# Recurrent layer: second column sums and GpSimd's output copies moved ahead in the order

## Chip, cores and metric

One NeuronCore of a Trainium2 chip runs the whole program in one launch. The metric is the device time of that launch in microseconds, the median of several runs. The profile is one execution of the same program; its page names the engines PE (TensorE), DVE (VectorE), ACT (ScalarE), POOL (GpSimd) and SP (SyncE, which here issues nearly all DMAs).

## The reference

The input is `x`, 128 sequences of 64 steps of 256 features, in float32, with a 64 x 64 adjacency. Four residual layers follow each other, each closed by a layer norm: a graph attention, a second graph attention over 512 edges, a graph layer with two batch norms, and the one that this case concerns, a recurrent layer over a two-step graph convolution:

```
h = relu(adj @ (x @ Wg0 + bg0)); h = relu(adj @ (h @ Wg1 + bg1))
for p in (1, 2, 3, 4):
    wins = windows of p successive steps of h          # 64 // p per sequence
    last = LSTM_p(wins, zero start state), last hidden state
    h[:, last step of each window] = last
x = layernorm(x + h)
```

An LSTM step has gates i, f, g, o, each 256 wide, from `x_t @ Wih.T + h @ Whh.T + bias`; `c = sigmoid(f) c + sigmoid(i) tanh(g)`, `h = sigmoid(o) tanh(c)`. Lengths p = 1 to 4 run one after the other on the same `h`, so each sees what the shorter ones wrote.

## The kernel before

**Tiling.** The recurrent layer handles the 128 sequences in eight groups of 16, two groups to a pair, four pairs one after the other (`k` = 0 to 3). A pair's activations are one tile `H` (128 partitions, two groups, two halves of the features, 64 steps, 16 sequences). `gcn` builds a pair's half-group of `H` in some eight steps, the last of which writes `H` (L1347, L1348).

**Products.** Where it can, the kernel computes a gate's 2 x 2 block product with seven products in place of eight, which needs sums of the inputs' blocks. For p = 1, `column_sums(n)` (L1389 to L1394) makes four such sums of group n, 128 x 512 each, on GpSimd, into the tile `Tn[n]`, which shares a buffer with weights (`wx`). `Wide` runs p = 1: gate g of group 0 takes all eight products (`eight`, L1505) and needs no sums; the other five gates take seven (`seven`, L1437), in the order 1, 6, 5, 2, 3, 7, then 4 during the next gate. Products 6, 7 and 4 share a bank of PSUM, so 7 cannot start before VectorE has read 6, nor 4 before it has read 7. The instructions that are issued through the helper `given` have its line, L116, in the profile. For p > 1, `Gate` does the same (L1700) with `hsums` and `xsums`; product uses are at L1711 to L1728, gates' activations at L1733, cell and hidden products at L1597 to L1622. Six banks (`l`) hold products on their way from TensorE to VectorE and ScalarE.

**Order.** `lstm` is a generator that yields numbered units: 0 to 7 for p = 1, 8 to 21 for p = 2, 22 to 32 for p = 3, 33 to 47 for p = 4. Beside it stands a table (`put`) of side work: at each unit the loop at the end (L1927 to L1930) advances the parts that are due there. Side parts are `gcn` of the next pair, `prepare` (loads of weights), and `final`. `given` ties each part's instructions behind those before it on each engine, so the order on an engine is nearly that of the text. In pairs 1 and 2, a layer norm of `gcn` for the pair after follows unit 0: on VectorE L1292 to L98, on GpSimd L86 and L100.

**Outputs.** `final(g, s)` turns step s (of every four) of group g into an output. For s = 0, 1, 2, which p = 4 does not write, it copies the columns with two GpSimd instructions into a tile `hd` (L1835), loads the residual rows (`x3r`, L1843), transposes blocks on VectorE (L1236 in `turned`), sends the result through DRAM (`way`, L1239, and back, L1241), and yields. Its second step, two units on, adds the residual (L1850), normalises and stores (L1860). The first steps stand at units 34, 36, 38, 40, 42, 44, the two groups in turn. For s = 3 the columns come straight from VectorE's last products (L1591).

[...]A transpose at L1236 is followed on VectorE by gate work, and a copy at L1835 on GpSimd by the forget gate's product with the cell (L1610) or by a layer norm (L86, L100).

Of the kernel before, what the change touches and what calls it, by code (L numbers as in the profile page):

```python
# [41 lines left out]
def kernel(ctx: ExitStack, tc: tile.TileContext, i, out):  # L42
# [45 lines left out]
    def layernorm(dst, src, n, engine):  # L88

        st = small.tile([P, n, 6], F32, name="ln_st", bufs=5)  # L90
        mv = small.tile([P, n, 2], F32, name="ln_mv", bufs=5)
        both = small.tile([P, 2, n], F32, name="ln_rs", bufs=5)
        rs, ng = both[:, 0, :], both[:, 1, :]
        for r in range(n):
            nc.vector.bn_stats(st[:, r, :], src[:, r, :])  # L95
            nc.vector.bn_aggr(mv[:, r, :], st[:, r, :])
        rsqrt(rs, mv[:, :, 1], n)
        nc.vector.tensor_scalar_mul(ng, mv[:, :, 0], -1.0)  # L98
        for r in range(n):
            engine.tensor_scalar(dst[:, r, :], src[:, r, :], ng[:, r:r + 1], rs[:, r:r + 1],  # L100
                                 op0=OP.add, op1=OP.mult)
# [8 lines left out]
    def given(do, *args, **more):  # L110
        traced = nc.cur_bb.bb.instructions
        first = len(traced)
        with ExitStack() as order:
            for e in latest.values():
                order.enter_context(tc.issue_after(e))
            r = do(*args, **more)  # L116
        for t in traced[first:]:
            if t.engine in (mybir.EngineType.PE, mybir.EngineType.DVE, mybir.EngineType.Activation,
                            mybir.EngineType.Pool):
                latest[t.engine] = t  # L120
        return r
# [8 lines left out]
    with ExitStack() as two:  # L130
# [450 lines left out]
        pair = su.tile([P, EC, 4], F32, name="pair")  # L581
# [154 lines left out]
        def hidden(q, m):  # L736
            return Z[q][:, m, :] if m < 2 else Aq(q)[:, (m - 2) * QT:(m - 1) * QT]
# [15 lines left out]
        def put(q, m, p_):  # L753
            nc.scalar.activation(hidden(q, m), p_, AF.Identity, bias=b1[:, m:m + 1])
            nc.vector.bn_stats(st1[:, m, q, :], hidden(q, m))
# [405 lines left out]
    def gbank(shape):  # L1161
        return ps.tile([P] + shape, F32, name="g", bufs=2)
# [69 lines left out]
    def turned(src):  # L1232


        t = work.tile([P, 4, 4, 32], F32, name="st", bufs=ST)
        nc.vector.transpose(t, src.rearrange("p n (j t) -> p j n t", t=32))  # L1236
        o = work.tile([P, 4, 4, 32], F32, name="st", bufs=ST)
        way = dram.tile([P, 4, P], F32, name="way", bufs=4)
        nc.sync.dma_start(way, t.rearrange("p j n f -> p j (n f)"))  # L1239
        for j in range(4):  # L1240
            nc.sync.dma_start(o[j * 32:(j + 1) * 32].rearrange("t i n f -> t i (n f)"),  # L1241
                              way[:, j, :].rearrange("(i t) x -> t i x", t=32))
        return o.rearrange("p i (c m) f -> p c m i f", m=KD)
# [132 lines left out]
    def lstm(pair):  # L1376
# [123 lines left out]
        def eight(G, rest):  # L1500

            def two(m, v):
                b = lbank([QT])
                for k in range(KD):
                    nc.tensor.matmul(b, G.weight(m, k), half(G.n, k, v), start=k == 0, stop=k == KD - 1)  # L1505
                return b

            for m in range(2):
                for v in range(2):
                    G.act(m, v, given(two, m, v))  # L1510
                    next(rest, None)
            for _ in rest:
                pass

        def seven(G, rest, order):
            for j in order:
                G.product(j)
                next(rest, None)
            for _ in rest:
                pass  # L1520

        rest = iter(())
        for n in range(2):
            if n == 0:
                given(column_sums, 0)
                yield "begin", 0
            gates = {}
            for name in "gio":
                if (n, name) == (0, "o"):
                    given(column_sums, 1)  # L1530
                G = Wide(name, n, gates)
                if name == "g" and n == 0:
                    eight(G, rest)
                    rest = iter(())
                else:
                    seven(G, rest, (1, 6, 5, 2, 7, 3) if (n, name) == (1, "o") else (1, 6, 5, 2, 3, 7))
                    rest = G.tail()
                if (n, name) == (1, "o"):
                    G.last()
                yield "at", unit  # L1540
                unit += 1
            yield "at", unit
            unit += 1

        for p in range(2, SKIP + 1):
# [197 lines left out]
            for r in range(len(runs)):  # L1743
                if p > 2:
                    yield "gap", unit
                for s in range(p):
# [16 lines left out]
                    else:  # L1763
# [31 lines left out]
                        o = prev  # L1795
# [32 lines left out]
    def final(g, s, pieces=1):  # L1828

        if s == SKIP - 1:  # L1830
            h = lasts.pop(g)
        else:
            h = late.tile([P, 2, KD, P], F32, name="hd", bufs=3)
            for c in range(2):
                nc.gpsimd.tensor_copy(h[:, c].rearrange("p k (w b) -> p k w b", b=GB),  # L1835
                                      Hs[g // 2][:, g % 2].rearrange("p k (c w s) b -> p c k w s b",
                                                                     c=2, s=SKIP)[:, c, :, :, s, :])

        rows = [v[g * GB:(g + 1) * GB].rearrange("b (c w s) d -> s c w b d", c=2, s=SKIP)[s]
                for v in (x3_dram, out_view)]  # L1840
        xr = work.tile([P, 2, D], F32, name="x3r")
        for c in range(2):
            nc.sync.dma_start(xr[:, c, :], rows[0][c])  # L1843
        for cs in ([(0, 1)] if pieces == 1 else [(0,), (1,)]):
            r = slice(cs[0], cs[-1] + 1)
            if pieces == 1:
                ht = turned(h.rearrange("p c m t -> p (c m) t"))
                yield
                xv = xr.rearrange("p c (m i f) -> p c m i f", m=KD, f=32)
                nc.vector.tensor_add(xv, ht, xv)  # L1850
            else:
                ht = gbank([2, D])
                for c in cs:
                    for k in range(KD):
                        nc.tensor.transpose(ht[:, c, k * P:(k + 1) * P], h[:, c, k], ident)
                nc.vector.tensor_add(xr[:, r], ht[:, r], xr[:, r])
            o = work.tile([P, 2, D], F32, name="st", bufs=ST)
            layernorm(o[:, r], xr[:, r], len(cs), nc.gpsimd)
            for c in cs:
                nc.sync.dma_start(rows[1][c], o[:, c, :])  # L1860
        yield
# [9 lines left out]
    for n in [0, 0, 0, 1, 1, 0, 1, 0, 0, 1, 2, 0, 0, 2, 1, 2, 1, 0, 3, 1, 1, 1]:  # L1871
        given(next, parts[n])
    lstms = [lstm(k) for k in range(NP)]
    next(lstms[0])
    for n in [2, 3, 2, 3, 2]:
# [18 lines left out]
    def gap(u):  # L1894
        return "gap", u

    def wait(u):
        return "wait", u

    for k in range(NP):  # L1900
        if k:
            put(k, prepare(weights_of[k, 3]), 8)
            put(k, prepare(weights_of[k, 4]), 23)
        else:
            put(k, prepare(weights_of[k, 4]), 23, 26, 30)
        for n in range(2):
            g = k * 2 + n
            for s in range(SKIP - 1):
                u = 34 + 4 * s + 2 * n
                put(k, final(g, s), u, u + 2)  # L1910
            if k < NP - 1:
                put(k + 1, final(g, SKIP - 1), 9 + n, 12 + n)
        if k < NP - 1:
            put(k, prepare(weights_of[k + 1, 2]), 34)
            for n, keys in enumerate([
                    [9, gap(11), 12, wait(15), 16, gap(18)],
                    [5, 9, 11, 13, 15, 19, wait(22), gap(22), gap(25), 26, gap(29)],
                    [13, 17, 19, 21, 23, 27, wait(33), gap(33), gap(36), 37, 38],
                    [21, 24, 26, 28, 30, 34, gap(40), 41, gap(44), 45, 46]]):
                block = gcn((k + 1) * 2 + n // 2, n % 2, gbank, "hT")  # L1920
                if n == 0 and k:
                    put(k - 1, block, 40, 42, 43)
                    put(k, block, 0, 0)
                elif n == 0:
                    put(k, block, 0, 1, 3, 5, 7)
                put(k, block, *keys)
# [5 lines left out]
    for n in (1, 0):  # L1932
        for _ in final((NP - 1) * 2 + n, SKIP - 1, pieces=2):
            pass
# [40 lines left out]
```

## Time and profile before

| | us |
|---|---|
| median of 3 runs | 2052.08 |
| lowest, highest | 2048.62, 2052.64 |
| profiled execution, its own time | 2051.53 |
| its span, first to last instruction | 2049.7 |
| TensorE busy | 1943.6 (95%) |
| VectorE busy | 1256.3 (61%) |
| ScalarE busy | 987.6 (48%) |
| GpSimd busy | 883.8 (43%) |

Pair 0's p = 1 starts at some 796 us of the span (its first column sum), pairs 1, 2 and 3 begin at 1133, 1445 and 1756 us. A line of a timeline gives start, duration, engine, source line, operation, the tile written and those read, the shapes, how many such instructions stand together, and in brackets how long the engine stood idle before it and what released it. A line of the waits gives who waited, for whom, the total in us, how often, and the longest. Two neighbouring matrix products overlap at their ends, so the time lost at a gap is read from start to start; the gap itself is a little shorter. Mean granted TensorE clock was 0.986 of full speed.

### The profile page before, as it was taken

What the parts mean: (1) busy time and instruction counts of PE and PEld (TensorE: products, weight loads), DVE (VectorE), ACT (ScalarE), POOL (GpSimd) and SP (SyncE); (2) the same over time, 40 slices, a digit from 0 to 9 for tenths busy, and PEclk for the clock granted to TensorE, in tenths of its full rate; (3) what the DMA queues carried; (4) which work ended last, traced back from release to release, by engine and by line L of the source; (5) the groups of instructions that cost most, each with busy time, mean ns of one, the idle gap of its engine ahead of it and who ended that gap; (6) DMA issues with size and microseconds to landing.
All of it is one profiled execution on the core that took longest, in us unless ns stands there. A gap on an engine that the chain in (4) does not pass through costs nothing.

```text
span 2049.7 us, 31505 instructions
## 1 busy us (share of the span) xinstructions
PE 1943.6 (95%) x11447; PEld 1332.9 (65%) x11447; DVE 1256.3 (61%) x2763; ACT 987.6 (48%) x1892; POOL 883.8 (43%) x1017
## 2 busy tenths in 40 slices
PE   5999999999899989899999999999999999999997
PEld 4666667766454435477677477677577667578685
DVE  7456665564457454765566865556775557764566
ACT  2766667666335633634343644343544333544333
POOL 1123334343345543564545543435443445444264
PEclk8999999999999999999999999999999999999998
DMA  5344443332112125432242243132143032131022
GB/s 134 79 65 68 79 69 54 66 50 39 37 29 60 41 103 171 158 136 98 112 143 85 77 140 139 42 126 91 52 153 120 21 113 65 44 119 78 0 65 70
DMA packets 236539, 173.84 MB, mean 85 GB/s; under 512 B 150624, under 2 KB 213600, under 8 KB 233056
## 3 DMA queue, kind: packets, MB, share of 16 engines
q1 hardware_dynamic: 234528, 169.86, 29.1%
q8 instruction: 90, 1.47, 0.3%
q0 software_dynamic: 1024, 1.05, 0.2%
q10 hardware_dynamic: 832, 0.92, 0.1%
q14 instruction: 65, 0.53, 0.1%
HBM read 110.18 MB, written 61.60 MB: 84 GB/s over the span
## 4 chain that ended last, share of the span: by engine, by line
PE 68%; DVE 17%; ACT 5%; POOL 4%; issue 4%; DMA 1%; SPq 0%; DVEq 0%; POOLq 0%; ACTq 0%
PE l L1700 25%; PE l L1656 7%; PE l L1437 4%; PE pz L820 4%; PE e L346 3%; PE m L318 2%; PE pz L749 2%; PE g L1336 2%; PE m L253 2%; PE m L321 2%; PE z L355 2%; PE pz L1017 2%; PE g L1324 2%; DVE ln_st L95 1%; DVE cell L1614 1%
## 5 line engine op out<-in xcount | busy, mean ns | idle before, releaser
L1700 PE MATMUL l<-xs,wx 128*128 128x256 f32 (+1 forms) x896 | 277.0, 400 | 5.7 <-DVE gate L1719 4.2
L1700 PE MATMUL l<-hs,wh 128*128 128x256 f32 (+1 forms) x896 | 276.5, 399 | 2.9 <-DVE hs L1564 2.1
L1715 ACT ACTIVATE kept<-l 128x256 f32<-128x256 f32 (+1 forms) x224 | 88.6, 402 | 332.2 <-PE l L1700 330.7
L86 POOL TENSOR_TENSOR ln_rs<-ln_rs,mhalf 128x2 f32<-128x2 f32 (+2 forms) x98 | 86.4, 882 | 338.1 <-DVE ln_rs L98 334.9
L1700 PE MATMUL l<-H,wx 128*128 128x256 f32 (+1 forms) x672 | 210.5, 402 | 4.3 <-DVE gate L1728 3.4
L1700 PE MATMUL l<-hid,wh 128*128 128x256 f32 (+1 forms) x672 | 208.8, 399 | 0.0
L1700 PEld LDWEIGHTS l<-xs,wx 128*128 128x128 f32 x896 | 168.6, 190 | 50.7 <-issue 5.8
L1700 PEld LDWEIGHTS l<-hs,wh 128*128 128x128 f32 x896 | 169.2, 190 | 46.8 <-DVE hs L1564 4.7
L1733 ACT ACTIVATE gate<-gate,bias 128x512 f32<-128x512 f32 (+1 forms) x280 | 170.6, 657 | 42.0 <-DVE gate L1724 34.8
L1656 PE MATMUL l<-H,wx 128*128 128x256 f32 (+5 forms) x672 | 185.2, 431 | 4.9 <-DVE H L116 2.7
L1656 PEld LDWEIGHTS l<-H,wx 128*128 128x128 f32 x672 | 118.8, 190 | 65.5 <-issue 34.2
L357 ACT ACTIVATE u<-z 128x1024 f32<-128x1024 f32 x128 | 130.3, 1025 | 63.4 <-PE z L355 62.6
L1700 PEld LDWEIGHTS l<-H,wx 128*128 128x128 f32 x672 | 125.7, 190 | 42.6 <-DVE gate L1728 7.4
L1700 PEld LDWEIGHTS l<-hid,wh 128*128 128x128 f32 x672 | 127.2, 190 | 32.0 <-issue 2.6
L1723 POOL TENSOR_TENSOR gate<-gate,kept 128x256 f32<-128x256 f32 (+1 forms) x84 | 64.9, 773 | 154.2 <-DVE kept L1721 153.9
L329 DVE TENSOR_TENSOR qs<-m,qs 64x256 fp32r<-64x256 f32 x128 | 54.1, 422 | 109.1 <-ACT qs L328 107.0
L355 PE MATMUL z<-gath_r,qs 128*128 128x512 f32 x256 | 99.9, 478 | 0.6 <-ACT u L357 0.4
L1622 ACT ACTIVATE gate<-cell 128x512 f32<-128x512 f32 (+1 forms) x88 | 58.6, 666 | 86.5 <-DVE cell L1614 64.5
L1568 POOL TENSOR_TENSOR hs<-hid 128x256 f32<-128x256 f32 (+1 forms) x28 | 27.4, 977 | 168.3 <-DVE hid L1600 85.2
L1728 DVE TENSOR_TENSOR gate<-l,gate 128x256 f32<-128x256 f32 (+1 forms) x112 | 50.0, 446 | 61.4 <-POOL gate L1723 36.4
L1610 POOL TENSOR_TENSOR cell<-gate,cell 128x512 f32<-128x512 f32 (+1 forms) x56 | 75.4, 1367 | 28.4 <-ACT gate L1733 28.4
L1717 DVE TENSOR_TENSOR gate<-l,kept 128x256 f32<-128x256 f32 (+1 forms) x112 | 49.2, 439 | 57.1 <-ACT gate L1733 32.9
(375 smaller groups left out, 4095.3 us busy)
## 6 DMA issues: line engine op xcount, KB each, us to landing
wx<-sums SPq DMA_DIRECT2D x9, 2048.0 KB
wh<-sums SPq DMA_DIRECT2D x9, 1792.0 KB
way<-st SPq DMA_DIRECT2D x54, 256.0 KB
st<-way SPq DMA_DIRECT2D x216, 64.0 KB
xin<-in_x SPq DMA_DIRECT2D x16, 512.0 KB
ld<-table SPq DMA_DIRECT2D x16, 512.0 KB
x_dram<-y SPq DMA_DIRECT2D x16, 512.0 KB
x2r<-x_dram SPq DMA_DIRECT2D x32, 256.0 KB
```

Source lines behind the costliest of these rows:

```text
L86: nc.gpsimd.tensor_tensor(dst, dst, mhalf[:, :n], OP.pow)
L346: nc.tensor.matmul(pes[S][n * CG:(n + 1) * CG, :], apad[:, k, CG - HEADS - r0:2 * CG - HEADS - r0], u[:, k, :], start=r0 == 0 and k == 0, ...
L355: nc.tensor.matmul(z[:, k, :], L1[q]["qs"][c][:, s, k * P:(k + 1) * P], gath_r, start=True, stop=True)
L357: nc.scalar.activation(u, z, AF.Relu)
L820: nc.tensor.matmul(self.bank[at], lhs, rhs, start=first and n == 0, stop=n == len(self.terms) - 1, skip_group_check=True)
L1437: nc.tensor.matmul(self.bank[at], lhs, rhs, start=new, stop=True, skip_group_check=True)
L1610: nc.gpsimd.tensor_tensor(c, t, c, OP.mult)
L1656: nc.tensor.matmul(b, w.raw[0][:, k, at, m, :], x, start=k == 0, stop=k == KD - 1)
L1700: nc.tensor.matmul(self.banks[j], lhs, rhs, start=src == 0, stop=src == 1)
L1715: nc.scalar.activation(self.keep(j), b, AF.Copy)
L1723: e.tensor_tensor(t[0][:, 1], t[0][:, 1], k[5], OP.add)
L1733: given(lambda: nc.scalar.activation(dst, dst, f, bias=b))
```

## The change

Two orders are changed; no instruction is added or taken away.

1. In pairs 1 to 3, the four column sums of the second group are issued directly behind those of the first, before gate g of the first group, where they stood before gate o. Pair 0 stays as it was.
2. `final` for s = 0, 1, 2 gets one more yield, behind the copies to `hd`. The copies now stand one unit ahead of the rest of the first step, at units 33, 35, 37, 39, 41 and 43.

```
         for n in range(2):
             if n == 0:
                 given(column_sums, 0)
+                if pair:
+                    given(column_sums, 1)
                 yield "begin", 0
             gates = {}
             for name in "gio":
-                if (n, name) == (0, "o"):
+                if (n, name) == (0, "o") and not pair:
                     given(column_sums, 1)
...
             for c in range(2):
                 nc.gpsimd.tensor_copy(h[:, c].rearrange("p k (w b) -> p k w b", b=GB),
...
+            yield
+
         rows = [v[g * GB:(g + 1) * GB].rearrange("b (c w s) d -> s c w b d", c=2, s=SKIP)[s]
...
                 u = 34 + 4 * s + 2 * n
-                put(k, final(g, s), u, u + 2)
+                put(k, final(g, s), u - 1, u, u + 2)
```

In the built program the order on TensorE, VectorE and ScalarE is the same as before. On GpSimd the column sums and the copies of outputs 2 to 6 of each pair have moved; those of output 1 have the same neighbours as before. On SyncE the DMAs of outputs 2, 4 and 6 stand in the order `way`, `x3r`, `x3r` instead of `x3r`, `way`, `x3r`.

More of the change, by code (lines that the diff above doesn't have):

```diff
@@ L1525, in lstm @@
                 given(column_sums, 0)
+                if pair:
+                    given(column_sums, 1)
                 yield "begin", 0
@@ L1528, in lstm @@
             for name in "gio":
-                if (n, name) == (0, "o"):
+                if (n, name) == (0, "o") and not pair:
                     given(column_sums, 1)
@@ L1837, in final @@
                                                                      c=2, s=SKIP)[:, c, :, :, s, :])
+            yield
         rows = [v[g * GB:(g + 1) * GB].rearrange("b (c w s) d -> s c w b d", c=2, s=SKIP)[s]
@@ L1909 @@
                 u = 34 + 4 * s + 2 * n
-                put(k, final(g, s), u, u + 2)
+                put(k, final(g, s), u - 1, u, u + 2)
             if k < NP - 1:
```

## The prediction

> **What bounds the kernel now.** I read the page first: TensorE is busy for almost the whole span, so a change elsewhere counts only where it lengthens or shortens one of TensorE's own gaps.
>
> ```profile
> PE 1943.6 (95%) x11447; PEld 1332.9 (65%) x11447; DVE 1256.3 (61%) x2763; ACT 987.6 (48%) x1892; POOL 883.8 (43%) x1017
> ```
>
> Next the waits of all engines, for the wait that the moved copies (L1835) cause, and then the waits of TensorE alone, after 750 us:
>
> ```profile
> DVE st L1236 <- POOL hd L1835: 41.8, 20, 3.3
> ```
> ```profile
> PE l L1437 <- DVE gate L116: 4.7, 5, 1.1
> ...
> PE l L1700 <- DVE gate L1719: 4.2, 6, 1.0
> PE l L1700 <- DVE gate L1728: 3.4, 8, 0.4
> ```
>
> VectorE stands 41.8 us for the copies, in 20 of 24 outputs. TensorE's waits for VectorE's recurrent work are a few us. So most of the 41.8 us is covered by TensorE's lead of six banks, and the question is which waits reach TensorE.
>
> I number a pair's outputs at units 34, 36, 38, 40, 42, 44 as 1 to 6. By the timeline, their waits in pair 0 are 0, 3.27, 0.47, 3.27, 0.94, 2.62 us; pairs 1 and 2 agree within 0.02, and pair 3 has 0.47 at output 5. The fifth, as VectorE's timeline and then TensorE's show it:
>
> ```profile
> 1097.61 0.71 DVE L1236 STREAM_TRANSPOSE st<-hd 128x512 f32<-128x512 f32 x1 [0.94 <-POOL hd L1835]
> ...
> 1103.32 0.69 DVE L1614 TENSOR_TENSOR cell<-cell,gate 128x512 f32<-128x512 f32 x1
> 1103.93 0.42 DVE L1719 TENSOR_TENSOR gate<-l,kept 128x256 f32<-128x256 f32 x1
> ...
> 1105.59 0.42 DVE L1728 TENSOR_TENSOR gate<-l,gate 128x256 f32<-128x256 f32 x1
> ```
> ```profile
> 1102.80 0.67 PE L1700 MATMUL l<-xs,wx 128*128 128x256 f32 x2 [0.24 <-POOL st L100]
> 1104.49 1.14 PE L1700 MATMUL l<-xs,wx 128*128 128x256 f32 x4 [1.02 <-DVE gate L1719]
> 1106.06 0.70 PE L1700 MATMUL l<-H,wx 128*128 128x256 f32 x2 [0.43 <-DVE gate L1728]
> ```
>
> After the wait VectorE runs without a further pause to L1728, and TensorE waits for banks that L1719 and L1728 empty. This wait reaches TensorE in full. At the third the chain to L1728 at 1075.51 has the same form. At the second, fourth and sixth VectorE catches up before TensorE runs out of banks, except in pair 3, which has no graph layer to run in between.
>
> The second part of the change concerns the start of pairs 1 to 3. GpSimd's column sums of the second group, then VectorE beside them, in pair 1:
>
> ```profile
> 1147.76 1.27 POOL L1391 TENSOR_TENSOR wx<-H 128x512 f32<-128x512 f32 x1
> 1148.98 1.72 POOL L1393 TENSOR_TENSOR wx<-H 128x512 f32<-128x512 f32 x1
> 1150.66 1.71 POOL L1392 TENSOR_TENSOR wx<-H,wx 128x512 f32<-128x512 f32 x1
> 1152.45 1.27 POOL L1394 TENSOR_TENSOR wx<-H,wx 128x512 f32<-128x512 f32 x1
> ```
> ```profile
> 1148.07 3.17 DVE L116 TENSOR_TENSOR cell<-cell,hid 128x512 f32<-128x512 f32 x2
> 1151.17 0.68 DVE L116 TENSOR_TENSOR wh<-l,wh 128x512 f32<-128x512 f32 x1
> ...
> 1152.63 2.24 DVE L116 TENSOR_TENSOR wh<-wh,hs 128x512 f32<-128x512 f32 x2 [0.19 <-ACT wh L116]
> 1154.80 0.68 DVE L116 TENSOR_TENSOR gate<-l,wh 128x512 f32<-128x512 f32 x1
> ```
>
> Products of two SBUF tiles, 0.69 us elsewhere, take one by one 1.50, 1.74 and 1.64 us, each ending 0.54 or 0.55 us after a column sum. The read from PSUM (wh<-l,wh) does not stretch. TensorE then waits 1.12 us for the last line shown, o's product 7, ahead of o's product 4; pairs 2 and 3 have the same 1.12. From start to start (1152.42 to 1155.53 where two products of 0.86 need 1.72) it loses 1.4 us.
>
> [...]Here four sums start 1.2 to 1.8 us apart, and one released by VectorE ends 1.13 us later (VectorE's 1134.85 to GpSimd's 1135.97). I use 1.13 for one sum behind a blocked turn.
>
> **Part 1, copies one unit ahead.** [...]On GpSimd, outputs 2, 4 and 6 are now copied right behind the hidden sums, ahead of the f gate's additions; 3 and 5 between the additions of g and i; 1 stays put. Two copies take 0.74 us. GpSimd idles before those additions for 3.24 us (1051.48), 1.83 and 1.09 (1111.43), and 2.57 to 2.77 before i's: the copies are hidden there; where the cover failed they would cost up to 0.74 each. They leave their old place in front of f's cell product (L1610), a small gain off the path.
> SyncE's DMAs for outputs 2, 4, 6 stand as way, x3r, x3r where before it was x3r, way, x3r. The x3r issue takes 0.62 us, so the transposed data leave about 0.6 to 0.7 us earlier and the addition at L1850, which moves up, stays covered by them.
> The gains, each the wait removed and no more than TensorE's loss behind it:
> - pairs 0, 1, 2: outputs 3 and 5, 0.47 + 0.94, 0.49 + 0.94, 0.47 + 0.94: 4.25 us. TensorE's losses from start to start there are at least 0.7 and 1.7, so they hold these.
> - pair 3: outputs 3 and 5, 0.47 each: 0.94. Outputs 2 and 4: TensorE waits for L1717 right behind the late transpose (0.49 and 0.50; from start to start 1967.41 to 1968.49 less 0.43, 0.65): 1.30.
> - output 6 of pair 3: L1850 at 2029.87 waits 1.14 us for data whose DMA stood behind the late transpose; with them 1 us earlier, its layernorm ends earlier and L1613 behind it (2031.74) can follow ScalarE's i gate (2030.95) at 2031.0. All of VectorE's work from there to the last outputs follows: 0.74.
> Sum 7.2 us. Bounds: 0 if something else ends those waits, 7.2[...].
>
> **Part 2, column sums.** No instruction is added; four of L1391 to L1394 in each of pairs 1 to 3 start at 1138.8 instead of 1147.8, ahead of two layernorms (L86, L100) in pairs 1 and 2. Behind them VectorE has, up to i's product 6:
>
> ```profile
> 1137.92 1.82 DVE L1591 TENSOR_TENSOR hd<-gate 128x256 f32<-128x256 f32 x3
> 1139.67 0.68 DVE L1292 TENSOR_TENSOR x2r<-st,x2r 128x512 f32<-128x512 f32 x1
> ...
> 1141.53 0.68 DVE L1292 TENSOR_TENSOR x2r<-st,x2r 128x512 f32<-128x512 f32 x1
> ...
> 1143.43 0.68 DVE L116 TENSOR_TENSOR cell<-l,wh 128x512 f32<-128x512 f32 x1
> ```
>
> Three of these have two SBUF inputs[...]: sum 1 starts when VectorE lets go at 1139.07, ends at 1140.20; the third hd product ends 0.28 later, 1140.48 (was 1139.41); sum 2 to 1141.61, the fourth hd product 1141.89; sum 3 to 1143.02, the first x2r addition to 1143.57 (was 1140.35). VectorE is 3.2 us late. Sum 4 ends at 1144.7, before the second addition. Product 6 is read at 1146.65 to 1147.35; product 7, in the same bank, was at 1144.62, with 0.5 us to spare: **TensorE stands 2.8 us**. GpSimd's layernorms end at 1149.05, about when its addition for product 7 has its data (1149.2), so no more comes from them; their stores (L1297) leave 3 us later too, and unit 9 is the first to use that buffer again. [...]two products that took 3.17 take 1.4, and o's product 7 is read about 1.8 us earlier against TensorE: the 1.4 us loss goes. Pairs 1 and 2: +2.8 - 1.4 each. Pair 3 has no layernorm there (its product 6 waits 2.47 us for TensorE), so only the gain: -1.4. Sum +1.4. Bounds: -4.2 if VectorE is not late, +8.6 as below.
>
> **Sum.** 7.2 - 1.4 = 5.8 us off. The profiled execution took 2051.53 (span 2049.7): 2045.7. The median, 2052.08, is 0.55 above it: 2046.3.
>
> **Rivals.**
> - *Only the gain in part 2*: [...]product 6 isn't late. For: VectorE was 0.5 us early. Against: strict turns at 1134 to 1139. 7.2 + 4.2: 2040.7.
> - *The copies' waits are covered anyway* and another releaser ends those stalls (products L1614, ScalarE's i gate, the DMA before L1850, which already ended a wait of 0.24 in pair 1): about 1.5 us of part 1 is left, part 2 costs 1.4. No change, 2052. Against: VectorE's pauses between transpose and L1728 sum to 0.28 us in every pair but that one.
> - *Slower*: [...]Each of four blocked by a sum at its longest, 1.72: 6.9, less 0.5 spare, 6.4 at product 7, twice, less 4.2: +8.6, less part 1's 7.2: 2053.5. It decides from 5.7 us at product 7 on ((7.2 + 4.2) / 2).
> - *The change doesn't do what it says*: the built order shows the moves, so no chance of its own.
>
> **Numbers.** Forecast 0.64, spread 2044 to 2049; rivals 0.11, 0.17, 0.08. The range takes in the second rival, leaving the first and third out: 2042.5 to 2052.5. Some 0.2%, 4.1 us, can be told from no change: faster (below 2048.0) from most of the forecast and the first rival, 0.65; same 0.31; slower 0.04.
>
> **What would show it.** Right: L1236's wait for hd gone; TensorE's wait for L1719 and L1728 roughly halved; in pairs 1 and 2 a new TensorE wait of 2 to 3 us at L1437 for VectorE's cell<-l,wh, and none of 1.12 in any pair. Wrong: L1236 waiting for DMA or TensorE instead; L1850 waiting for st<-way; L1723 late on GpSimd; no stall at product 7.

## The result, and the profile after

The changed kernel takes 2047.13 us, the median of 15 runs (2044.94 to 2050.21); the kernel before, run beside it, 2051.28 (15 runs, 2048.32 to 2052.64). The ratio on record, which is not the quotient of the two medians, is 0.9983, 95% interval 0.9976 to 0.9991: some 3.5 us faster, between 1.8 and 4.9. The forecast of 2046.3 is 0.8 us from the median. That closeness is in part luck. The gain was forecast as 5.8 us, which lies above the whole interval; and the kernel before was 0.8 us faster in these runs than in the three from which the forecast started, which brings the two times together.

The profiled execution of the changed kernel has a span of 2044.6 us, 5.1 less than before. That difference must not be read as the change's: 2.7 us of it lie ahead of the recurrent layer, where the two programs are the same (its first product starts at 798.05 instead of 800.76 us, and over all profiles of this study between 798 and 804). So every profile below is read by stretches of one pair: A from the first product of gate g (L1505) to the first plain product of p = 2 (L1658, before L1656); B from there to the first plain product of p = 4; C from there to the next pair's first product, or to the end. In us:

| pairs 0, 1, 2, 3 | A | B | C |
|---|---|---|---|
| before | 56.83, 39.21, 39.20, 39.20 | 175.21, 171.95, 171.94, 148.28 | 100.56, 100.91, 99.99, 105.65 |
| after | 56.84, 40.36, 41.76, 37.20 | 175.20, 171.95, 171.94, 148.27 | 99.32, 99.84, 98.78, 105.04 |
| difference | 0.0, +1.15, +2.56, -2.00 | 0 | -1.24, -1.07, -1.21, -0.61 |

Part 1, the copies, is column C: 4.1 us gained. Part 2, the column sums, is column A: 1.7 us lost. Together 2.4 us, within the interval of the timed runs.

The page's busy times don't tell that anything has changed: the shares are 95% for TensorE, 61% for VectorE and 43% for GpSimd, as before. From the waits of all engines (who, for whom, total us, times, longest):

```profile
DVE gate L1730 <- POOL gate L1725: 59.9, 38, 3.4
```

VectorE's wait of 41.8 us for the copies is gone: in none of the 24 outputs does L1236 wait for `hd`. But more than half of it has only moved: VectorE's wait for GpSimd's gate additions (L1725, before L1723) was 36.4 us and is 59.9. At output 2 of pair 1, for one, the transpose had waited 3.27 us and the use of the addition behind it (L1728) 0.74; now the transpose doesn't wait and the use (L1730) waits 3.15, since VectorE reaches it sooner than GpSimd is done. TensorE's wait for that use doesn't grow by it; it is 3.4 us as before. TensorE's waits after 750 us are

```profile
PE l L1437 <- DVE cell L116: 5.5, 2, 2.9
...
PE g L1859 <- DVE hd L1593: 3.7, 1, 3.7
PE l L1702 <- DVE gate L1730: 3.4, 8, 0.4
...
PE l L1702 <- DVE gate L1721: 3.3, 5, 1.1
...
PE l L1437 <- DVE gate L116: 1.3, 2, 0.8
```

The first line is new, the stall at product 7 in pairs 1 and 2. The last has lost its three gaps of 1.12 us. The tail (L1859, before L1855), the products behind the last output's transposes, waits 3.7 instead of 4.3 us. L1721 (before L1719) has one case less, but its longest is 1.1: in pairs 0 to 2 its waits have fallen from 3.3 to 1.2 us, while two in pair 3 have grown from 0.46 and 0.45 to 1.10 and 1.01.

**The stall at product 7.** GpSimd and then VectorE at the start of pair 1:

```profile
1134.80 1.45 POOL L1391 TENSOR_TENSOR wx<-H 128x512 f32<-128x512 f32 x1
1136.20 1.46 POOL L1393 TENSOR_TENSOR wx<-H 128x512 f32<-128x512 f32 x1
1137.62 1.46 POOL L1392 TENSOR_TENSOR wx<-H,wx 128x512 f32<-128x512 f32 x1
1139.15 1.60 POOL L1394 TENSOR_TENSOR wx<-H,wx 128x512 f32<-128x512 f32 x1
```
```profile
1133.96 3.98 DVE L1593 TENSOR_TENSOR hd<-gate 128x256 f32<-128x256 f32 x3
1137.87 1.75 DVE L1292 TENSOR_TENSOR x2r<-st,x2r 128x512 f32<-128x512 f32 x1
...
1140.80 0.68 DVE L1292 TENSOR_TENSOR x2r<-st,x2r 128x512 f32<-128x512 f32 x1
...
1142.98 0.69 DVE L116 TENSOR_TENSOR cell<-l,wh 128x512 f32<-128x512 f32 x1 [0.19 <-issue]
```
```profile
1139.71 1.12 PE L1437 MATMUL l<-H,wh 128*128 128x512 f32 x2
1143.72 1.12 PE L1437 MATMUL l<-wx,wh 128*128 128x512 f32 x2 [2.90 <-DVE cell L116]
```

Three products of two SBUF tiles, which took 1.82 us before, take 3.98, the first addition of L1292 1.75 instead of 0.68, and the second, which starts at 1140.80 when the last sum has just ended (1140.75), 0.68 again. So the read of product 6 (the last VectorE line) comes late, counted from the pair's first product by 3.5 us, of which the stretched instructions make up 3.2, and TensorE stands 2.90 us; 2.60 in pair 2. GpSimd itself isn't what is late: behind the sums its layer norm (L86, at 1140.91) waits 0.15 us for VectorE.

**Two outputs of pair 0.** Output 5's transpose and TensorE behind it:

```profile
1093.66 0.70 DVE L1236 STREAM_TRANSPOSE st<-hd 128x512 f32<-128x512 f32 x1
```
```profile
1100.54 1.14 PE L1702 MATMUL l<-xs,wx 128*128 128x256 f32 x4 [0.42 <-DVE gate L1721]
1102.11 1.13 PE L1702 MATMUL l<-H,wx 128*128 128x256 f32 x4 [0.43 <-DVE gate L1730]
```

The wait of 0.94 us is gone, and TensorE's gaps of 0.24 and 1.02 are one of 0.42. At output 3 the gap at L1730 has kept its 0.43 us. ScalarE's gate, and VectorE's product that needs it; last, the same product before:

```profile
1066.86 0.71 ACT L1735 ACTIVATE gate<-gate,bias 128x512 f32<-128x512 f32 x1
```
```profile
1066.44 1.03 DVE L1347 TENSOR_SCALAR H<-g 128x512 f32<-128x512 f32 x1
1067.61 0.82 DVE L1615 TENSOR_TENSOR gate<-gate 128x512 f32<-128x512 f32 x1
```
```profile
1070.60 0.68 DVE L1613 TENSOR_TENSOR gate<-gate 128x512 f32<-128x512 f32 x1
```

The gate ends at 1067.57 and the product starts at 1067.61. Before, the product started 0.3 us behind the same gate (1070.29). Of the 0.47 us no more than 0.3 could be had, and as the product now takes 0.82 us instead of 0.68, 0.15 is left for TensorE.

**Pair 3.** VectorE at output 3, TensorE some units later, and SyncE's DMAs ahead of it; last, SyncE's before:

```profile
1969.09 0.70 DVE L1236 STREAM_TRANSPOSE st<-hd 128x512 f32<-128x512 f32 x1
1970.88 0.69 DVE L1854 TENSOR_TENSOR x3r<-st,x3r 128x512 f32<-128x512 f32 x1 [1.09 <-DMA st<-way]
```
```profile
1976.64 1.14 PE L1702 MATMUL l<-xs,wx 128*128 128x256 f32 x4 [1.10 <-DVE gate L1721]
```
```profile
1961.65 1.37 SPq L1864 DMA_DIRECT2D out<-st  x2
1963.12 0.41 SPq L1239 DMA_DIRECT2D way<-st  x1
1963.58 1.28 SPq L1847 DMA_DIRECT2D x3r<-x_dram  x2
1967.50 1.73 SPq L1241 DMA_DIRECT2D st<-way  x4
```
```profile
1966.19 1.37 SPq L1860 DMA_DIRECT2D out<-st  x2
1967.66 0.62 SPq L1843 DMA_DIRECT2D x3r<-x_dram  x1
1968.33 0.47 SPq L1239 DMA_DIRECT2D way<-st  x1
1968.85 0.62 SPq L1843 DMA_DIRECT2D x3r<-x_dram  x1
1971.57 1.73 SPq L1241 DMA_DIRECT2D st<-way  x4
```

L1854, the addition of output 2, now comes before its data, and what stands behind it on VectorE waits with it: the gate product (L1615) starts at 1972.76, while ScalarE's gates were done at 1972.00. TensorE's gap of 0.49 us at 1968 is gone, and the next one has grown from 0.46 to 1.10. Before, the same `way` was issued 2.13 us behind the first store and its read back 3.24 us after that; here 1.47 and 4.38. The issue moved up by 0.7 us, the landing, as the issue of the read back shows it, not at all: 5.4 us from store to read back before, 5.8 here.

Two kinds of transfer stand around `way` here, the stores (`out`) ahead of it and the reads of the residual (`x3r`) beside it. The graph layer of the kernel before has the same write of 256 KB behind two stores of 128 KB, in pair 2 without a read, in pair 1 with one:

```profile
1584.26 1.10 SPq L1297 DMA_DIRECT2D x_dram<-A  x2
1586.02 0.32 SPq L1239 DMA_DIRECT2D way<-st  x1
1588.07 1.74 SPq L1241 DMA_DIRECT2D st<-way  x4
```
```profile
1272.19 1.10 SPq L1297 DMA_DIRECT2D x_dram<-A  x2
1273.39 0.39 SPq L978 DMA_DIRECT2D x2r<-x_dram  x1
1273.95 0.32 SPq L1239 DMA_DIRECT2D way<-st  x1
1277.34 1.74 SPq L1241 DMA_DIRECT2D st<-way  x4
```

Without the read it is back 2.05 us after its issue, with the read 3.39. All twelve profiles have it so: 2.05 or 2.06 in pair 2, 3.3 to 3.7 in pairs 0 and 1. So stores ahead don't delay such a write in every case, and a read beside it goes with a delay. In the outputs the stores never come without `x3r`; which of the two holds `way` there, these profiles can't tell.

### The profile page after: what moved, and what is told of

It reads as the page before. It is cut to its first block, busy times and chain, and to the rows that moved or that the text cites. A ratio compares the mean times of both kernels' runs of the same rounds, so it can differ in the third digit from the quotient of the medians.

```text
span 2044.6 us, 31490 instructions
## 1 busy us (share of the span) xinstructions
PE 1938.6 (95%) x11447; PEld 1333.7 (65%) x11447; DVE 1255.5 (61%) x2763; ACT 987.7 (48%) x1892; POOL 881.6 (43%) x1017
## 3 DMA queue, kind: packets, MB, share of 16 engines
q8 instruction: 90, 1.47, 0.3%
## 4 chain that ended last, share of the span: by engine, by line
PE 69%; DVE 17%; ACT 5%; issue 3%; POOL 2%; DMA 2%; SPq 1%; DVEq 0%; ACTq 0%; POOLq 0%
PE l L1702 27%; PE l L1658 7%; PE l L1437 5%; PE pz L820 4%; PE pz L749 3%; PE e L346 3%; PE m L318 2%; PE g L1336 2%; PE pz L1017 2%; PE g L1324 2%; PE m L321 2%; PE z L355 2%; DVE cell L1616 2%; PE m L253 2%; DVE ln_st L95 2%
## 5 line engine op out<-in xcount | busy, mean ns | idle before, releaser
L86 POOL TENSOR_TENSOR ln_rs<-ln_rs,mhalf 128x2 f32<-128x2 f32 (+2 forms) x98 | 86.4, 882 | 335.9 <-DVE ln_rs L98 335.3
L1658 PE MATMUL l<-H,wx 128*128 128x256 f32 (+5 forms) x672 | 185.2, 431 | 4.9 <-DVE H L116 2.7
L1658 PEld LDWEIGHTS l<-H,wx 128*128 128x128 f32 x672 | 118.8, 190 | 65.5 <-issue 34.2
L1725 POOL TENSOR_TENSOR gate<-gate,kept 128x256 f32<-128x256 f32 (+1 forms) x84 | 65.0, 774 | 145.1 <-DVE kept L1723 144.8
L1730 DVE TENSOR_TENSOR gate<-l,gate 128x256 f32<-128x256 f32 (+1 forms) x112 | 50.0, 446 | 87.8 <-POOL gate L1725 59.9
L1719 DVE TENSOR_TENSOR gate<-l,kept 128x256 f32<-128x256 f32 (+1 forms) x112 | 49.1, 438 | 60.1 <-ACT gate L1735 33.0
```

Of the source, the lines that this page charges most:

```text
L86: nc.gpsimd.tensor_tensor(dst, dst, mhalf[:, :n], OP.pow)
L1658: nc.tensor.matmul(b, w.raw[0][:, k, at, m, :], x, start=k == 0, stop=k == KD - 1)
L1725: e.tensor_tensor(t[0][:, 1], t[0][:, 1], k[5], OP.add)
```

## The experiments

Each edit is against the changed kernel, and the stretches come from each kernel's own profile.

### Each part alone

The copies alone; the column sums stand as before:

```
-                if pair:
-                    given(column_sums, 1)
-                if (n, name) == (0, "o") and not pair:
+                if (n, name) == (0, "o"):
```

> The copies of outputs one unit ahead, the column sums where they stood before. A stretch of p = 1 is read from the pair's first product of gate g to the first product of p = 2, a stretch of p = 4 from its first plain product to the next pair's start or the end of the span. Theory: the two parts do not touch each other. The stretches of p = 1 in pairs 1, 2, 3 go back to 39.2 us each, those of p = 4 stay where the changed kernel has them (99.3, 99.8, 98.8, 105.0, against 100.6, 100.9, 100.0, 105.7 before), so 4.2 us off the time before, about 2047. Rival: the parts lean on each other (a pair that starts earlier finds its sums earlier), and p = 4 gains less than half of that, 2 us off or less.

Measured: 2048.41 us, ratio 0.9982 (0.9976 to 0.9989). A as before (39.21, 39.20, 39.21); C 99.32, 99.32, 98.78, 104.58, a gain of 5.1 us by the profile and 3.7 (2.3 to 4.9) by the times. In pair 1 it is 0.5 us better than the changed kernel, where at output 3 the addition L1854 stands idle for 0.82 us before it starts and TensorE keeps a gap of 0.34 us. The profile shows no releaser for that wait; before, at the same place, it was 0.24 us for `st<-way`. In pair 3 `st<-way` ends waits of 0.69, 1.01 and 0.66 us, as in the changed kernel (1.09, 1.00 and 0.56).

The sums alone:

```
-                put(k, final(g, s), u - 1, u, u + 2)
+                put(k, final(g, s), u, u, u + 2)
```

> The column sums early in pairs 1 to 3, the copies where they stood before. Theory: p = 1 takes 40.4 us in pairs 1 and 2 (41.8 in pair 2 if the clock is throttled again) and 37.2 in pair 3, p = 4 as before, so 0.3 to 1.7 us slower than before, not told apart from it by the clock on the wall; TensorE waits 2.6 to 2.9 us for VectorE ahead of product 7 in pairs 1 and 2. Rival: the early sums pay over the whole layer because later work starts from a better place, 1 us or more faster than before.

Measured: 2055.36 us, ratio 1.0013 (1.0006 to 1.0019), 2.7 us slower where at most 1.7 was expected. A 41.77, 41.78, 37.20; TensorE stands 2.61 and 2.62 us at product 7. C as before, but for 0.3 us more in pair 3. So the stall comes of the sums and not of the copies, and the first part pays for the second. Both stalls cost as much as pair 2's in the changed kernel; why pair 1's was cheaper there is seen below.

The early sums in the last pair only, which has no layer norm of a next pair at its start:

```
-                if pair:
+                if pair == NP - 1:
                     given(column_sums, 1)
...
-                if (n, name) == (0, "o") and not pair:
+                if (n, name) == (0, "o") and pair < NP - 1:
```

> The change, with the early column sums in the last pair alone. Theory (the layer norm of the graph layer behind the sums is what makes them dear, and only pairs 1 and 2 have it there): p = 1 takes 39.2, 39.2, 37.2 us, p = 4 as in the changed kernel, so 6 us off the time before and 2 to 4 off the changed kernel, about 2044 to 2045. Rival (the gain of pair 3 came from the pairs before it): pair 3 gains nothing, 39.2, and the time is that of the copies alone, about 2047.

Measured: 2046.23 us, ratio 0.9968 (0.9959 to 0.9977). A 39.21, 39.22, 37.20; C 99.33, 99.68, 98.79, 105.36. What helps in pair 3 is kept, and what hurts in pairs 1 and 2 is left away. That is 6.6 us (4.7 to 8.4) off the time before, as expected.

### The order of the transfers

All three steps of an output at their units, but the transposes, with the DMA to `way`, ahead of the layer norm and stores of the output before:

```
+        ends = []
...
-                put(k, final(g, s), u - 1, u, u + 2)
+                ends.append((final(g, s), u + 2))
+                put(k, ends[-1][0], u - 1, u)
...
+        for part, u in ends:
+            put(k, part, u)
```

> The change, with the transpose of outputs 2, 4 and 6 issued ahead of the earlier output's layer norm and stores instead of behind them, so that the way DMA stands ahead of those stores. Theory (pair 3's gain was lost to a wait for the transposed data, 1.09 us at outputs 3 and 5, because the way DMA lands behind the stores of the output before it, 5.3 to 6.0 us after the first of them however early it is issued): the addition of the residual waits for no DMA, way lands about 2 us after its issue, and pair 3's p = 4 takes 103 us instead of 105.0; pairs 0 to 2 stay within 0.3. Rival (ScalarE's gate would have ended the wait there, too): pair 3's p = 4 stays within 0.5 of 105.0.

Measured: 2047.02 us, ratio 0.9976 (0.9969 to 0.9983). C 99.32, 99.32, 98.78, 102.12: pair 3 gains 3.5 us where the changed kernel gained 0.6. A 40.06 and 40.32 in pairs 1 and 2, with stalls of 2.60 and 2.86 us at product 7. The three waits of L1854 for `st<-way` in pair 3, 2.65 us together, are gone, and pair 3's C is 2.9 us shorter than the changed kernel's. So the late data account for most of what pair 3 had lost. The edit moves the transposes on VectorE, the stores and the reads of `x3r` at once; what the new place on VectorE does by itself, and which of the transfers had made the data late, it doesn't show. The profile gains 7.6 us in all, the times 4.9 (3.5 to 6.4); the section on the sum comes back to that.

The copies early for the first group's outputs alone (1, 3, 5), with the sums as before (the first edit above, and this):

```
-                put(k, final(g, s), u - 1, u, u + 2)
+                put(k, final(g, s), u - 1 if n == 0 else u, u, u + 2)
```

> The kernel before with one part of the copies alone: only the first group's outputs (1, 3, 5) have their copies a unit early, the second group's (2, 4, 6) stay, the column sums too. Theory (in pairs 0 to 2 the gain is outputs 3 and 5 alone, VectorE catches up after 2, 4 and 6): the stretch of the plain products falls from 100.6, 100.9, 100.0 to 99.3, 99.3 to 99.8, 98.8 us in pairs 0 to 2, as with all copies; in pair 3 the last output's tail is not shortened, 105.2 to 105.7 us instead of 104.6. Rival (outputs 2, 4 and 6 take part): half of the gain or less in pairs 0 to 2.

Measured, one profiled run of 2046.09 us: C 99.37, 99.98, 98.82, 104.72. Pairs 0 to 2 have about all of the gain that they have in the changed kernel from outputs 3 and 5, as worked out (pair 1 has 0.9 us of it, where the copies alone gave 1.6). In pair 3 the theory was right on the tail, whose gap is 4.14 us (before 4.29, after 3.71), and wrong on the sum, 104.72 instead of 105.2 or more. From a gap of 1.16 or 1.17 us late in pair 3's p = 3, which these kernels share (at 1910.62 here), to the start of the tail's gap TensorE takes 118.31 us, before 119.13, with all copies alone 118.64, in the changed kernel 119.05. So outputs 3 and 5 gave 0.8 of the 0.94 forecast for them. With the copies of 2 and 4 early as well, 0.3 of that was lost, in the changed kernel nearly all; each is one profile.

### What the sums collide with

In place of the second group's sums in pairs 1 to 3, GpSimd instructions that only write:

```
         def column_sums(n):
             T, e = Tn[n], nc.gpsimd
+            if n and pair:
+                for j in range(8):
+                    e.memset(T[:, j // 2], 0.0)
+                return
```

> The changed kernel, but in pairs 1 to 3 the second group's column sums are replaced, at the same early place, by eight GpSimd writes of constants to the same buffers, each of one half of a sum's output, which read nothing. It leaves out the second group's column sums in those pairs. Theory[...]: VectorE's hd products and x2r additions there take 0.69 to 1.1 us and are not drawn out, TensorE doesn't stand 2.9 and 2.6 us at product 7, and a pair's first stretch (from its first product to the first plain product) takes some 37.2 us in pairs 1, 2 and 3, against 40.4, 41.8 and 37.2. Rival (the stall comes of GpSimd's time: layernorm and its addition for product 7 come later behind whatever stands ahead of them): the stall stays at 2 to 3 us and the stretches at 40 us and more in pairs 1 and 2.

Measured, one run: A 37.20, 37.20, 37.19; C as after. GpSimd and VectorE at the start of pair 1:

```profile
1135.21 3.82 POOL L1393 MEMSET wx<- 128x512 f32 x8
```
```profile
1134.40 1.82 DVE L1597 TENSOR_TENSOR hd<-gate 128x256 f32<-128x256 f32 x3
1136.15 0.68 DVE L1292 TENSOR_TENSOR x2r<-st,x2r 128x512 f32<-128x512 f32 x1
```

While GpSimd writes for 3.82 us, the same VectorE instructions take their plain time, 1.82 us for the three products and 0.68 for the addition; beside the sums, which read SBUF, they took 3.98 and 1.75. The writes take 2.1 us less of GpSimd's time than the sums, so this run alone doesn't exclude that GpSimd's time plays a part. The changed kernel's own trace does: there GpSimd, when the sums are done, waits for VectorE, and VectorE, for which TensorE waits, is late almost wholly by the stretched instructions, 3.2 of 3.5 us.

The sums left early, and the graph layer's normalisation (L1292 and what follows) put from unit 0 to unit 8:

```
-                    put(k, block, 0, 0)
+                    put(k, block, 8, 8)
```

> The changed kernel, with the graph layer's normalisation of the pair before put at unit 8 in place of unit 0, so that VectorE's hd products and x2r additions don't meet the early column sums. Theory (what the early sums cost is their meeting with these very instructions): the stall at product 7 is gone, the first stretch of pairs 1 and 2 takes 37.2 us as pair 3's does, about 7.7 us less in the two together; some of it may come back in the next stretch (171.9 us), where the additions then stand among the recurrent work: a time of 2040 to 2045 us. Rival (any VectorE work there is late, since GpSimd's sums stand in the way of the additions for product 7 themselves): 40 us and more in the first stretches, and a time of 2047 or more.

Measured: 2054.77 us, ratio 1.0022 (1.0014 to 1.0029). A 37.20, 37.20, 37.20, as forecast, though the three products of L1593 still meet the sums:

```profile
1135.56 3.97 DVE L1593 TENSOR_TENSOR hd<-gate 128x256 f32<-128x256 f32 x3
1139.86 0.69 DVE L116 TENSOR_TENSOR cell<-l,wh 128x512 f32<-128x512 f32 x1 [0.34 <-PE l L1437]
```

Two stretched products alone are covered; the stretched products and two additions with their statistics are not. But B grew to 178.67 and 179.34, and the expected time was missed by 10 us and more. TensorE in pair 1:

```profile
1178.82 0.46 PE L1254 MATMUL g<-bdT,A 64*64 64x64 f32 x16 [2.68 <-POOL A L100]
1180.38 0.46 PE L1254 MATMUL g<-bdT,A 64*64 64x64 f32 x16 [1.10 <-POOL A L100]
1181.70 1.24 PE L1254 MATMUL g<-bdT,A 64*64 64x64 f32 x32 [0.86 <-POOL A L100]
```

The graph layer's products at unit 9 wait for the normalisation, which is only one unit old. Some 4.6 of the 6.7 us that pair 1's B grew are these gaps. Around the last of them the granted clock falls to half, for 3.4 us in pair 1 and 6.8 us in pair 2; in pair 1 that is 1.7 us of work, most of the rest.

### Versions that go further

Transposes first, and the early sums in the last pair only (both edits above together):

> All copies early, the early column sums in the last pair alone, and the transposes, with the DMA that they start, of a unit's output issued ahead of the layernorm and the stores of the output before. Theory (each part's stretches add up, since they lie in different stretches): 39.2, 39.2 and 37.2 us in the first stretches of pairs 1 to 3, 99.3, 99.3, 98.8 and 102.1 in those of the plain products; against the kernel before -2.0 and -7.6, a sum of 9.6 us, a ratio of about 0.9953. Rival (the shorter stretches are given back at the next one, or the spread before the recurrent layer hides them): 0.997 as with the early sums in the last pair and the copies alone.

Measured: 2041.68 us, ratio 0.9957 (0.9943 to 0.9971). A 39.22, 39.21, 37.20; C 99.32, 99.32, 98.78, 102.44: -2.0 and -7.3 us, a sum of 9.2 before rounding; the times (8.8, between 5.9 and 11.7) agree. The parts add up. SyncE and VectorE in pair 3:

```profile
1955.23 0.34 SPq L1239 DMA_DIRECT2D way<-st  x1
1957.26 1.73 SPq L1241 DMA_DIRECT2D st<-way  x4
1959.09 1.39 SPq L1864 DMA_DIRECT2D out<-st  x2
1960.58 1.27 SPq L1847 DMA_DIRECT2D x3r<-x_dram  x2
```
```profile
1966.23 0.70 DVE L1236 STREAM_TRANSPOSE st<-hd 128x512 f32<-128x512 f32 x1
1966.85 0.65 DVE L1854 TENSOR_TENSOR x3r<-st,x3r 128x512 f32<-128x512 f32 x1
```

With the stores and the reads of `x3r` behind it, the same 256 KB are back for reading 2.03 us after their issue, not 4.38, and L1854 follows the transpose without a wait.

Transposes first, early sums in all pairs, and the normalisation at unit 3, between the sums and its use:

```
-                    put(k, block, 0, 0)
+                    put(k, block, 3, 3)
```

> The changed kernel with the transposes of an output issued ahead of the layernorm and stores of the output before, and the graph layer's normalisation of pairs 1 and 2 at unit 3 in place of unit 0: behind the early column sums (they end some 9 us after the pair's start) and well ahead of its first use at unit 9. Theory: the first stretches take 37.2 us in all of pairs 1 to 3 and the next ones keep their 171.9 us; with 99.3, 99.3, 98.8 and 102.1 us for the plain products that is 13 to 14 us less than before, a ratio of 0.993 to 0.994. Rival (VectorE and GpSimd have no room at unit 3 either, the products there wait as they did at product 7): 39 us and more in the first stretches, or the 6 to 7 us of the later place come back in the next ones.

Measured: 2040.95 us, ratio 0.9958 (0.9945 to 0.9972). A 39.53, 39.53, 37.20, where 37.2 was expected: the rival held. VectorE's additions at unit 3 stand among those of the second group's products, and in pair 1 two gaps of 0.9 us (TensorE at L1437 for VectorE's `hid` and `hs`, L116) take the place of one of 2.9. The same at unit 2:

> As the kernel with the normalisation at unit 3, at unit 2. Theory: the same, 37.2 us in the first stretches and 171.9 in the next. Rival: at unit 2 VectorE has the additions of the first group's o gate to make and is late for the second group's first product: 38 us and more in the first stretches of pairs 1 and 2.

Measured, one run of 2040.43 us: A 39.53, 39.53, 37.20, the same two gaps. That is 0.5 and 0.8 us less than at unit 0 with the transposes first (40.06, 40.32), but 0.3 us more in each pair than with the late sums (39.21, 39.20): at neither unit do the additions fit in without making products late. The normalisation at unit 3 can't be told by its ratio from the version with the early sums in the last pair only; the intervals of both lie below the changed kernel's.

## Why the prediction was right, and where its sum was off

**The signs that it had named.** Of the signs of being right three came: no wait for `hd`, a new stall of 2 to 3 us at product 7, and no gap of 1.12. The fourth didn't: TensorE's wait for L1719 fell from 4.2 to 3.3 us only and that for L1728 stayed at 3.4. Of the signs of being wrong two came: L1854 (its L1850) waits for `st<-way`, which is the failed step below, and VectorE waits longer for GpSimd's additions (its L1723), which did not reach TensorE.

**The stall at product 7: right, and its size too.** Forecast 2.8 us in pairs 1 and 2, none in pair 3; measured 2.90, 2.60 and none. The turns between the sums and VectorE were worked out from those of the first group's sums in the kernel before:

```profile
1133.18 1.38 POOL L1391 TENSOR_TENSOR wx<-H 128x512 f32<-128x512 f32 x1 [2.68 <-PE l L1700]
1134.52 1.45 POOL L1393 TENSOR_TENSOR wx<-H 128x512 f32<-128x512 f32 x1
1135.93 1.45 POOL L1392 TENSOR_TENSOR wx<-H,wx 128x512 f32<-128x512 f32 x1
1137.46 1.33 POOL L1394 TENSOR_TENSOR wx<-H,wx 128x512 f32<-128x512 f32 x1
```
```profile
1134.33 0.51 DVE L1723 TENSOR_TENSOR gate<-gate,kept 128x256 f32<-128x256 f32 x1
1134.77 1.48 DVE L1724 TENSOR_TENSOR gate<-kept 128x256 f32<-128x256 f32 x1
...
1136.83 0.83 DVE L1591 TENSOR_TENSOR hd<-gate 128x256 f32<-128x256 f32 x1 [0.24 <-ACT gate L1733]
```

By these lines each of the three VectorE instructions ends 0.28 us behind a sum, and the next sum 1.13 us behind it. That the second group's sums would go on so was the author's estimate, and they did: three VectorE instructions were drawn out (two of L1593, from 0.41 to 1.49 us each, and the first addition, from 0.68 to 1.75), and the last sum stood beside instructions that kept their time. The rival with a fourth instruction drawn out fell, and so did the one in which VectorE isn't late.

**What the stall costs: not its length alone.** In A pair 1 lost 40.36 - 37.20 = 3.16 us for a gap of 2.90, but pair 2 41.76 - 37.20 = 4.56 for one of 2.60. The granted clock of TensorE in pair 2, us by us (the third figure from the end):

```profile
1456.00:1457.00 1.00, 1.00 (x3) 0.50 (x2) 0.39 (x2) 0.00 (x0) 0.90 (x3) 0.69 0.54 179
1457.00:1458.00 1.00, 1.00 (x2) 0.37 (x2) 0.63 (x1) 0.00 (x0) 0.47 (x2) 0.50 0.86 260
1458.00:1459.00 1.00, 1.00 (x2) 0.34 (x1) 0.00 (x0) 0.36 (x1) 1.00 (x1) 0.50 0.92 282
1459.00:1460.00 1.00, 1.00 (x3) 0.38 (x2) 0.00 (x0) 0.85 (x2) 0.04 (x1) 0.60 0.63 216
```

Half clock for 0.62 + 1 + 1 + 0.8 = 3.4 us, that is 1.7 us of lost work (the clock was whole until 1456); 4.56 - 2.60 - 1.7 leaves 0.26, what pair 1 has beside its gap. The drop doesn't follow every stall: of six stalls at product 7, those of 2.60, 2.61 and 2.62 us (the changed kernel's pair 2 and the two with the sums alone) were followed by the drop, and those of 2.60, 2.86 and 2.90 us (the two with the transposes first and the changed kernel's pair 1) were not. So their length alone doesn't decide; what does, these runs don't show. The prediction had no term for it.

**The gap ahead of o's product 4: right, a little small.** Forecast -1.4 in each pair, measured -2.0 (39.20 to 37.20). The two pairs of products behind the old gap, from start to start, had taken 1.06 and 1.10 us (1155.53, 1156.59, 1157.69) where other pairs, 1.02 from start to end, take 0.86 from start to start; that is 0.4 of the 0.6 that a reading of the gap alone missed; the rest stays open.

**Part 2's sum came out by luck.** The stalls cost 3.16 + 4.56 us for the 5.6 forecast, 2.1 more, and the three gaps gave 6.0 for 4.2, 1.8 more. The two errors nearly cancel: 1.7 us lost, 1.4 forecast.

**The copies: the waits right, the sum too large.** Part 1 was given 7.2 us and brought 4.1 in the profile of the changed kernel. Two terms were off.
- Pairs 0 to 2: forecast 4.25, measured 3.5 (4.05 with the copies alone). Output 5 gave 1.06 to 1.08 us for the 0.94 forecast. Output 3 gave 0.15 in pairs 0 and 2, for 0.47: ScalarE's gate comes right behind, and the product that waited for it took 0.14 us longer. In pair 1 it gave nothing for 0.49, as L1854 stood idle 0.82 us there. The prediction had named ScalarE's gate as a releaser, but only in a rival, and didn't ask how long after the gate the product had started.
- Pair 3: forecast 2.98, measured 0.61. The failed step is "the transposed data leave about 0.6 to 0.7 us earlier and the addition at L1850, which moves up, stays covered by them". They did leave earlier, by 0.7 us; they didn't land earlier, with the stores of the output before and the reads of `x3r` around them. The addition then waited 1.09, 1.00 and 0.56 us and took back what the copies gave: of the 0.61 us, 0.58 are the shorter tail (4.29 to 3.71, for 0.74 forecast), and outputs 2 to 5 gave next to nothing for 2.24. This is the second rival's mechanism, the DMA before L1850, in pair 3 and, as it seems, at output 3 of pair 1. Whether the stores or the reads delay the data stays open.

With the transposes issued ahead of the stores, C gives -1.24, -1.59, -1.21, -3.21 in one kernel and -3.53 as its last in the other: 7.25 and 7.6 us for the 7.2 forecast. In sum the stalls were priced nearly right, output 5 too low and output 3 too high; the transfers around one DMA stood in the wrong order.

**The sum.** 7.2 - 1.4 was forecast; the profile has 4.1 - 1.7 = 2.4, and the times 3.5 with an interval from 1.8 to 4.9. One clock drop more or less is 1.7 us, so the two don't contradict each other. How often it comes in the timed runs can be estimated from their mean granted clocks: 0.9857 for the kernel before (62 runs), and, of 20 runs each beside it, 0.9853 with the copies alone, 0.9844 with the sums alone, 0.9848 with the transposes first. A drop of 1.7 us is 0.0008 of the whole, so these are some 0.5, 1.6 and 1.1 drops in a run more than before. That is near the two drops in the profile of the sums alone, and it would explain about 2 us of the 2.7 by which the transposes first gained less in the times than in the profile, which has no drop in the recurrent layer.

## What to carry to other kernels

An earlier issue need not be an earlier arrival: when a DMA moves up, look at the transfers just ahead of it and beside it, and at how long the same transfer takes with and without them elsewhere in the trace (here 2.05 us alone behind stores, 3.4 with a read beside it). Before crediting the removal of a wait, find the second latest input of the waiting instruction and its distance; here 0.3 us of ScalarE's gate capped a gain of 0.47. And before moving GpSimd work that reads SBUF, look at what VectorE has beside and behind it: a use of a product in PSUM (L1728, at 1133.63) took 0.41 us beside a sum (0.41 to 0.51 in all of its cases), while the three products of two SBUF tiles went from 1.82 to 3.98. That lateness was covered in pair 3, where the early sums gained 2.0 us; where the layer norm's additions follow, they lost up to 2.6, of which 1.7 is the clock drop.

## What the runs showed of the hardware that had not been expected

- A 256 KB write to DRAM could be read back 2.03 us after its issue with the stores and reads behind it (outputs, transposes first), 2.05 us behind two stores of 128 KB with no read beside it (graph layer, pair 2), 3.39 us with a read of 256 KB between (pair 1), and 3.2 to 4.4 us with two stores ahead and two reads of 128 KB beside it (outputs in pair 3 before and after).
- A stall of TensorE of 2.6 us cost some 2.9 us in one case and 4.6 in three, those with 3.4 us at half clock after it.
- Writes by GpSimd, 3.82 us in a row, left VectorE's three products at 1.82 us together and the addition at 0.68, where sums that read drew them out to 3.98 and 1.75.
